# The second half of a gated MLP, and the down projection behind it, one tick later in a hand-ordered selective-scan block

## The chip, the cores and the metric

The kernel runs on one core of a Trainium2 chip. The metric is the device time of one execution in microseconds (us). The core has five engines that matter here: PE (TensorE, matmuls), DVE (VectorE), ACT (ScalarE), POOL (GpSimd) and SP (SyncE, which issues nearly all DMAs). Each engine executes its own instructions strictly in the order in which the program gives them; the engines meet only at semaphores.

## What is computed

The input `x` is 4 sequences of 1024 rows of 256 numbers, all in float32. The block is

```python
x = x + attn(layernorm(x))          # "attn" is a selective-scan (Mamba) layer with its own MLP
x = x + ffn(layernorm(x))

def attn(h0):                       # rmsnorm inside
    h   = h0 + mamba(rmsnorm(h0, n1))
    xn  = rmsnorm(h, n2)
    return h + (silu(xn @ gate.T) * (xn @ up.T)) @ down.T     # gate, up: 704 wide

def mamba(u):                       # z, x, B, C, dt_raw = split(u @ in_proj.T)
    dt = softplus(dt_raw @ dt_proj.T + b)
    state = exp(dt * A) * state + (dt * x) * B                # one step per row, 8 x 32 x 32 states
    y     = sum over states of state * C
    return ((y + x * D) * silu(z)) @ out_proj.T

def ffn(x):                         # 1024 wide; fwht is a Hadamard transform
    return fwht(silu(x @ W1.T) * (x @ W3.T)) @ W2.T
```

The Hadamard transform is folded into `W2` once, at the start of the kernel.

## The kernel before

**Units, steps and ticks.** The work is cut into 8 units of 512 rows (two to a sequence; the second carries the scan's state on). A unit's scan takes 16 steps `q`, each with four scans of 128 partitions by 512 time steps, and each step takes two *ticks*. So a unit is scanned for 32 ticks, and the 8 units are scanned one after the other without a break. What comes before a unit's scan (`pre`: norms, projections, the DMAs that spread dt and dt*x over the partitions) and what follows it (`post`: output projection, the gated MLP, the second norm, the ffn) is laid beside the scans of the units around it.

**What sets the order.** Nothing is scheduled by a planner. `at(tick, lane, fn)` (L264) puts a piece of work in a list, and the loop at L938 to L981 runs through the ticks and empties the lists lane by lane. Within one tick the order of emission is: lane `PE`; lane `ACT`; DVE's product bx = (dt*x)*B (`times_b`, L838); lane `ACTb`; two exponentials `exp` on ACT (L808), for scans two ticks ahead; a scan (L847); lane `DVE`; the second scan; lane `POOL0`; on even ticks POOL's product with C (`times_c`, L860, 4.5 us each); lane `POOL`; on odd ticks the sums over states on PE (`sum_states`, L871: four matmuls that collapse the partitions into the PSUM tile `py`); lane `PEend`; lane `ACTend`; then the DMAs on SP. "Behind the tick's sums" thus means lane `PEend`.

**The sums.** A group of 8 steps accumulates in the one PSUM tile `py`. The group starts with a matmul of x with a diagonal D (L869) and ends when ACT copies `py` out to `yt` (L889); as there is one `py`, the next group's L869 waits for that copy.

**The part that the change touches.** Let F be the tick at which `post` of a unit bases its MLP; the first six units ("many") have F = 33 + 32 times their number. Their MLP runs beside the scan of the next unit:

- F+9, F+10: transposes of the normed rows, `ht` (L239, L246).
- `gated` (L271) computes three 128-wide chunks of silu(gate)*up: gate matmuls for three chunks (`pg`), then one projection `z` of a later unit, then up matmuls (`pu`), two pieces of PE work a tick; `silus` on ACT one tick after the first matmuls (three silus and the one of `z`, with a change of the activation table before and after), copies `up` of the up results one tick later (L296), products on POOL one tick later (L300). A chunk is 128 columns of gate or up; the last is 64 wide and its gate and up come out of one matmul.
- The first three chunks enter at F+10, the second three at F+13 (L718 to L720).
- F+16 to F+22: projections of a later unit that lie in between: C's first half (`pe_c`, emitted at F+16, copied out by ACT as `cc`, L475, at F+17), dt (L447, F+18, lane `PEend`, then softplus on ACT, L456, F+19), C's second half (F+21).
- `down` (L721 to L728, by `add_rows`, L323): four row blocks of 128 rows, each an identity matmul that brings the residual `hr` (L336) and six matmuls over the chunks (L338). They stand at F+18, F+19, F+20 and F+21 in lane `PE`. After the second and after the fourth, ACT copies the sum back to `hr` (`replace`, L352) and takes the norm's statistics (`row_stats`, L193 and L196).
- F+23 to F+26: POOL turns the statistics into a scale (`small3`, L671 and the lines around), ACT norms the rows (`hn`, L226, F+24), PE transposes them (F+25), ACT copies them as `xt`, and the ffn's matmuls begin (F+26).

The six units take different tiles of the same pools: four PSUM banks `dense` for all matmul results but `py`, one SBUF tile each for the MLP's and the ffn's products. A matmul into a `dense` bank waits until the engine that reads the bank's last content is through.

A scan tile `da` is loaded by DMA (dt, spread), overwritten by ACT's exponentials, by DVE's scan and by POOL's product, and read by PE's sums. There are five; the DMA for step q+3 goes to the tile of step q-2, so it waits for that step's sums.

Of the kernel before, what the change touches and what calls it, by code (L numbers as in the profile page):

```python
# [27 lines left out]
def tile_block(ctx: ExitStack, tc: tile.TileContext, a, out):  # L28
# [195 lines left out]
    def scaled_rows(dst, src, scale, bias, ts):  # L224
        for t in ts:
            nc.scalar.activation(  # L226
                dst[:, t, :],
                src[:, t, :],
                AF.Identity,
                bias=bias[:, t : t + 1] if bias is not None else 0.0,  # L230
                scale=scale[:, t : t + 1],
            )
# [15 lines left out]
    def project(w, col, n, src, dst=None):  # L248
        if dst is None:
            dst = dense_psum()  # L250
        for k in range(2):
            nc.tensor.matmul(  # L252
                dst[:n],
                lhsT=w[:, k, col : col + n],
                rhs=src[:, k, :],
                start=(k == 0),
                stop=(k == 1),
            )
        return dst
# [4 lines left out]
    def at(tick, lane, fn, *args):  # L264
        todo[tick][lane].append(partial(fn, *args))
# [5 lines left out]
    def gated(tick, u, dst, wa, wb, chunks, src, z=None):  # L271


        g = [{} for _ in chunks]
        pe_z, act_z = z[0]["z"] if z else (None, None)

        def pe(i, name, w):
            c, n = chunks[i]
            if n < P:

                both = project(W[w], c * P, 2 * n, u[src])
                g[i]["pg"], g[i]["pu"] = both, both[n:]
            else:
                g[i][name] = project(W[w], c * P, n, u[src])

        def silus():
            for i, (_, n) in enumerate(chunks):
                g[i]["si"] = p3.tile([P, T], F32, tag="si", name="si")
                nc.scalar.activation(g[i]["si"][:n], g[i]["pg"][:n], AF.Silu)  # L289
            if z:  # L290
                act_z(z[1])

        def up(i):
            n = chunks[i][1]
            g[i]["up"] = p3.tile([P, T], F32, tag="up", name="up")
            nc.scalar.copy(g[i]["up"][:n], g[i]["pu"][:n])  # L296

        def product(i):
            c, n = chunks[i]
            nc.gpsimd.tensor_tensor(u[dst][c][:n], g[i]["si"][:n], g[i]["up"][:n], ALU.mult)  # L300

        three = len(chunks) == 3
        steps = [(i, *s) for s in (("pg", wa), ("pu", wb)) for i in range(len(chunks))]
        steps = [s for s in steps if chunks[s[0]][1] == P or s[1] == "pg"]
        late = z and len(steps) == 6
        steps = [(pe, *s) for s in steps]
        if z:
            steps.insert(3, (pe_z, z[1]))
        for k, step in enumerate(steps):
            at(tick + k // 2, "PE", *step)  # L310
        at(tick + 1, "ACTend" if three else "ACT", silus)
        at(tick + 2, "ACTend" if z else "ACT", up, 0)
        for i in range(1, len(chunks)):
            if i == 2 and late:
                at(tick + 3, "ACT", up, i)
            else:
                at(tick + 2, "ACTend", up, i)
        at(tick + 3 if z else tick + 2, "POOL", product, 0)
        for i in range(1, len(chunks)):

            at(tick + 3, "POOL" if three or u is not us[-2] else "POOL0", product, i)
# [325 lines left out]
    def post(u, E, other):  # L647


        s = {}  # L650
        last = u is us[-1]

        many = us.index(u) < len(us) - 2

        def hr(ts):
            if 0 in ts:
                u["hr"] = p2.tile([P, TT, DM], F32, tag="hr", name="hr")
            scaled_rows(u["hr"], u["x"], u["r1"], u["nm1"], ts)

        def small2():  # L660
            t = sm.tile([P, 2, TT], F32, tag="s2", name="s2")
            r3 = t[:, 1, :]
            rsqrt_eps(r3, u["mv"][:, 1, :])
            s["r3"] = r3

        def small3():
            t = sm.tile([P, 2, TT], F32, tag="s2", name="s2")
            nm, r4 = t[:, 0, :], t[:, 1, :]
            nm16, var = u["mv"][:, 0, :], u["mv"][:, 1, :]
            rsqrt_eps(r4, var)  # L670
            nc.gpsimd.tensor_tensor(nm, nm16, r4, ALU.mult)  # L671
            nc.gpsimd.tensor_scalar(nm, nm, 16.0, None, ALU.mult)
            s["r4"], s["nm"] = r4, nm

        def hn(scale, bias):
            s["tok"] = p1.tile([P, TT, DM], F32, tag="tok", name="hn")
            scaled_rows(s["tok"], u["hr"], s[scale], s[bias] if bias else None, range(TT))

        def big(name):
            if last:  # L680

                k = NQ + (1 if name == "m" else 3)
                tiles = [das[i % 5] for i in (k, k + 1)]
                u[name] = [tiles[c // 4][:, c % 4, :] for c in range(8)]
            else:
                tile = p1.tile([P, 8, T], F32, tag="big", name=name)
                u[name] = [tile[:, c, :] for c in range(8)]

        def store(lo=0, n=TT):
            b, first = u["b"], u["c"] * T + lo * P  # L690
            nc.sync.dma_start(
                out=out[b, first : first + n * P, :].rearrange("(t p) d -> p t d", p=P),
                in_=u["hr"][:, lo : lo + n, :],
            )

        at(E + 3, "ACT", hr, (0, 1))
        at(E + 4, "ACT", hr, (2, 3))
        add_rows(
            (E + 3,) * TT,
            u,  # L700
            lambda: [u["yt"][:, k, :] for k in range(2)],
            lambda: [W["wo"][:, k, :] for k in range(2)],
            "PEend",
            way="pool" if many else None,
        )
        for i in range(2):
            at(E + (5 + i if many else 4), "ACTend", row_stats, u, "hr", (2 * i, 2 * i + 1), False)

        F = E + 1 if many else E - 2
        at(E + 7 if many else E + 5, "POOL", small2)  # L710
        at(F + 8, "ACT", hn, "r3", None)
        at(F + 9, "PE", lambda: transposes(u, s["tok"]))
        at(F + 9, "ACTend", transposed, u, "ht")
        at(F + 9, "POOL", lambda: nc.gpsimd.tensor_tensor(u["hr"], u["hr"], u["x"], ALU.add))
        at(F + 10, "PE", big, "m")
        sizes = [min(P, DFF - c * P) for c in range(6)]
        chunks = list(enumerate(sizes))
        for i in range(2):  # L718
            gated(F + 10 + 3 * i, u, "m", "wg", "wu", chunks[3 * i : 3 * i + 3], "ht",
                  (other, i) if other else None)  # L720
        down = (18, 19, 20, 21) if many else (17, 17, 18, 18)  # L721
        add_rows(
            [F + t for t in down],
            u,
            lambda: [u["m"][c][:n] for c, n in enumerate(sizes)],
            lambda: [W["wd"][:n, c, :] for c, n in enumerate(sizes)],
            way="pe",
        )  # L728
        at(F + down[1] + 1, "ACTend", row_stats, u, "hr", (0, 1))
        if last:  # L730
            at(F + down[3] + 1, "DVE", row_stats_vector, u, "hr", (2, 3))
        else:
            at(F + down[3] + 1, "ACTend", row_stats, u, "hr", (2, 3))
        at(F + down[3] + 2, "POOL", small3)
        if not many:
            F -= 3
        at(F + 24, "ACTend" if many else "ACT", hn, "r4", "nm")
        at(F + 25, "PE", lambda: transposes(u, s["tok"]))
        at(F + 25, "ACTend", transposed, u, "xt")
        at(F + 26, "PE", big, "g")  # L740
        chunks8 = [(c, P) for c in range(8)]
        for i in range(3):
            gated(F + 26 + 3 * i, u, "g", "w1", "w3", chunks8[3 * i : 3 * i + 3], "xt")

        o2 = (E + 31, E + 36, E + 50, E + 50) if not (many or last) else range(F + 36, F + 40)
        add_rows(
            o2,
            u,
            lambda: u["g"],
            lambda: [w2h[:, c, :] for c in range(8)],  # L750
            way=None if last else "pool",
        )
        if last:
            at(o2[1] + 1, "SPend", store, 0, 2)
            at(o2[3] + 1, "SPend", store, 2, 2)
        else:
            at(o2[3] + 6, "SPend", store)
# [142 lines left out]
    for k, u in enumerate(us):  # L900
        post(u, 32 * k + 32, us[k + 2] if k + 2 < len(us) else None)
# [148 lines left out]
```

## Time and profile before

| | us |
|---|---|
| median of 3 runs | 1126.01 (1125.77 to 1127.81) |
| the profiled execution's own time | 1129.06 |
| its span, from the first to the last instruction | 1127.3 |
| PE busy with matmuls | 980.5 (87%) |
| DVE busy | 943.9 (84%) |
| POOL busy | 882.8 (78%) |
| ACT busy | 805.0 (71%) |
| mean granted clock of PE | 0.925 |
| bx of tick F of units 0 to 6, from the start | 153, 276, 399, 525, 646, 772, 895 |

A fp32 matmul leaves two records, so a group of four matmuls shows as x8. "Busy" says how long an engine had work in it; what matters for the end is which engine makes another one wait, stage by stage. A line of the timeline gives the start and the length of a run of like instructions, and in brackets how long the engine had been idle before it and whose semaphore ended that. Times in it are from the span's start.

### The profile page before, as it was taken

What the parts mean: (1) busy time and instruction counts of PE and PEld (TensorE: products, weight loads), DVE (VectorE), ACT (ScalarE), POOL (GpSimd) and SP (SyncE); (2) the same over time, 40 slices, a digit from 0 to 9 for tenths busy, and PEclk for the clock granted to TensorE, in tenths of its full rate; (3) what the DMA queues carried; (4) which work ended last, traced back from release to release, by engine and by line L of the source; (5) the groups of instructions that cost most, each with busy time, mean ns of one, the idle gap of its engine ahead of it and who ended that gap; (6) DMA issues with size and microseconds to landing.
All of it is one profiled execution on the core that took longest, in us unless ns stands there. A gap on an engine that the chain in (4) does not pass through costs nothing.

```text
span 1127.3 us, 12518 instructions
## 1 busy us (share of the span) xinstructions
PE 980.5 (87%) x3470; PEld 474.4 (42%) x3470; DVE 943.9 (84%) x813; ACT 805.0 (71%) x1443; POOL 882.8 (78%) x512
## 2 busy tenths in 40 slices
PE   7656246979999799989998999979998999898998
PEld 3121012333644345443644354433644363434555
DVE  4899799999989999899999999899989989894000
ACT  3956456887869796888779796979777777584331
POOL 6767668878998899888988899878988788685222
PEclk9777558989999899989999899989999999898999
DMA  7999998998998989998998989899999978760000
GB/s 236 375 363 347 319 377 313 327 317 309 306 342 298 351 302 316 320 333 300 319 347 309 343 284 338 307 337 310 314 321 323 325 255 315 264 223 1 1 19 19
DMA packets 108390, 321.94 MB, mean 286 GB/s; under 512 B 11488, under 2 KB 22176, under 8 KB 108320
## 3 DMA queue, kind: packets, MB, share of 16 engines
q1 hardware_dynamic: 106464, 318.39, 80.8%
q10 hardware_dynamic: 1856, 2.75, 0.7%
q8 instruction: 28, 0.46, 0.2%
q14 instruction: 42, 0.34, 0.1%
HBM read 302.22 MB, written 18.87 MB: 285 GB/s over the span
## 4 chain that ended last, share of the span: by engine, by line
PE 44%; ACT 12%; DMA 7%; DVE 5%; POOL 4%; issue 4%; SPq 0%; DVEq 0%; ACTq 0%; POOLq 0%
PE dense L252 27%; PE dense L338 11%; ACT da L808 5%; DMA da<-dtd 4%; PE py L871 4%; DVE da L847 3%; POOL da L860 3%; DMA ub<-ud 2%; DVE bx L838 2%; ACT up L296 1%; ACT un L226 1%; ACT hr L226 1%; PE dense L336 1%; ACT junk L196 1%; ACT junk L193 1%
## 5 line engine op out<-in xcount | busy, mean ns | idle before, releaser
L860 POOL TENSOR_TENSOR da<-da,cr 128x2048 f32<-128x2048 f32 x128 | 579.2, 4526 | 41.4 <-DVE da L847 19.1
L808 ACT ACTIVATE da<-da,nega 128x512 f32<-128x512 f32 x508 | 335.7, 715 | 72.9 <-DMA da<-dtd 67.3
L838 DVE TENSOR_TENSOR bx<-ub,pb 128x1024 f32<-128x1024 f32 x254 | 312.2, 1229 | 28.5 <-ACT pb L825 11.7
L847 DVE TENSOR_TENSOR_SCAN da<-da,carry,bx 128x512 f32<-128x512 f32 x256 | 313.9, 1267 | 22.0 <-ACT da L808 6.1
L847 DVE TENSOR_TENSOR_SCAN da<-da,bx 128x512 f32<-128x512 f32 x256 | 298.5, 1207 | 17.0 <-DVE bx L838 3.0
L252 PE MATMUL dense<-xt,w 128*128 128x512 f32 x512 | 241.8, 626 | 7.9 <-ACT xt L246 7.9
L871 PE MATMUL py<-da,rsel 128*32 128x512 f32 x1024 | 155.7, 670 | 83.7 <-POOL da L860 83.7
L252 PEld LDWEIGHTS dense<-xt,w 128*128 128x128 f32 x512 | 99.1, 200 | 146.9 <-issue 114.2
L296 ACT COPY up<-dense 128x512 f32<-128x512 f32 x112 | 63.4, 578 | 56.5 <-PE dense L252 56.3
L338 PE MATMUL dense<-w2h,g 128*128 128x256 f32 x448 | 102.1, 383 | 1.2 <-ACT ut L246 1.2
L871 PEld LDWEIGHTS py<-da,rsel 128*32 128x32 f32 x1024 | 23.8, 112 | 179.0 <-POOL da L860 118.4
L338 PEld LDWEIGHTS dense<-w2h,g 128*128 128x128 f32 x448 | 83.5, 190 | 24.2 <-issue 10.4
L300 POOL TENSOR_TENSOR g<-si,up 128x512 f32<-128x512 f32 x56 | 71.0, 1274 | 28.1 <-ACT up L296 28.1
L252 PE MATMUL dense<-ut,win 128*128 128x512 f32 x192 | 92.7, 614 | 0.2 <-ACT ut L246 0.2
L252 PE MATMUL dense<-ht,wg 128*128 128x512 f32 x192 | 87.6, 600 | 3.0 <-ACT ht L246 3.0
L338 PE MATMUL dense<-wd,m 128*128 128x256 f32 x336 | 85.7, 397 | 3.3 <-POOL m L300 3.3
L289 ACT ACTIVATE si<-dense 128x512 f32<-128x512 f32 x112 | 61.9, 595 | 34.9 <-PE dense L252 34.5
L252 PE MATMUL dense<-ht,wu 128*128 128x512 f32 x160 | 73.9, 601 | 1.8 <-ACT si L289 1.8
L300 POOL TENSOR_TENSOR m<-si,up 128x512 f32<-128x512 f32 (+1 forms) x42 | 52.6, 1274 | 26.1 <-ACT up L296 26.1
L338 PEld LDWEIGHTS dense<-wd,m 128*128 128x128 f32 x336 | 63.2, 195 | 21.2 <-issue 9.3
L808 ACT ACT_TABLE_LOAD x46 | 59.0, 1283 | 0.8
L252 PEld LDWEIGHTS dense<-ut,win 128*128 128x128 f32 x192 | 36.8, 197 | 52.5 <-issue 41.0
(110 smaller groups left out, 884.4 us busy)
## 6 DMA issues: line engine op xcount, KB each, us to landing
da<-dtd SPq DMA_DIRECT2D x254, 512.0 KB
ub<-ud SPq DMA_DIRECT2D x254, 512.0 KB
cr<-cd SPq DMA_DIRECT2D x64, 256.0 KB
x<-in_x SPq DMA_DIRECT2D x8, 512.0 KB
dtd<-dt SPq DMA_DIRECT2D x16, 256.0 KB
ud<-du SPq DMA_DIRECT2D x16, 256.0 KB
cd<-cc SPq DMA_DIRECT2D x16, 256.0 KB
xr<-xbd SPq DMA_DIRECT2D x60, 64.0 KB
```

What stands on the lines that cost most here:

```text
L193: nc.scalar.activation(junk, src[:, t, :], AF.Identity, scale=-1.0 / (16 * DM), accum_out=nm)
L226: nc.scalar.activation(dst[:, t, :], src[:, t, :], AF.Identity, bias=bias[:, t : t + 1] if bias is not None else 0.0, scale=scale[:, t : t ...
L252: nc.tensor.matmul(dst[:n], lhsT=w[:, k, col : col + n], rhs=src[:, k, :], start=(k == 0), stop=(k == 1),)
L289: nc.scalar.activation(g[i]["si"][:n], g[i]["pg"][:n], AF.Silu)
L296: nc.scalar.copy(g[i]["up"][:n], g[i]["pu"][:n])
L300: nc.gpsimd.tensor_tensor(u[dst][c][:n], g[i]["si"][:n], g[i]["up"][:n], ALU.mult)
L338: nc.tensor.matmul(dst, lhsT=left[k][:, t * P : (t + 1) * P], rhs=right[k], start=(k == 0 and way != "pe"), stop=(k == n - 1),)
L808: nc.scalar.activation(da, da if q else s["u"]["pdt", b], AF.Exp, scale=an[:, s["h"], s["j"], b, s["g"] : s["g"] + 1],)
L838: nc.vector.tensor_tensor(s["bx"], s["ub", b0 // 2], u["pb"].unsqueeze(1).broadcast_to([P, 2, T]), ALU.mult)
L847: nc.vector.tensor_tensor_scan(da, da, s["bx"][:, b % 2, :], start, ALU.mult, ALU.add)
L860: eng.tensor_tensor(da, da, s["cr"].unsqueeze(1).broadcast_to([P, n, T]), ALU.mult)
L871: nc.tensor.matmul(u["py"][32 * b : 32 * b + 32, :], lhsT=rsel[:, 2 * s["j"] + s["g"], :], rhs=s["da"][:, b, :], start=False, stop=last,)
```

## The change

In the six units with `many`, the second three chunks of the gated MLP enter at F+14 instead of F+13; with them their silus, copies and products and the `z` projection move by one tick. `down`'s row blocks stand at F+19, F+20, F+20 and F+21 instead of F+18, F+19, F+20 and F+21, and in lane `PEend` instead of `PE`. What follows from the ticks in `add_rows` and below moves too: the first `replace` and its statistics go from F+20 to F+21; the second stays at F+22. The last two units are as they were.

```diff
         for i in range(2):
-            gated(F + 10 + 3 * i, u, "m", "wg", "wu", chunks[3 * i : 3 * i + 3], "ht",
+            gated(F + 10 + (4 if many else 3) * i, u, "m", "wg", "wu", chunks[3 * i : 3 * i + 3], "ht",
                   (other, i) if other else None)
-        down = (18, 19, 20, 21) if many else (17, 17, 18, 18)
+        down = (19, 20, 20, 21) if many else (17, 17, 18, 18)
         add_rows(
             [F + t for t in down],
             u,
             lambda: [u["m"][c][:n] for c, n in enumerate(sizes)],
             lambda: [W["wd"][:n, c, :] for c, n in enumerate(sizes)],
+            "PEend" if many else "PE",
             way="pe",
         )
```

The order of the instructions that results, on the four engines' queues and on SP:

- PE, before: pu of chunk 2, pg of chunks 3, 4, 5, z, sums (F+14), pu 3 and 4, C, sums (F+16), row block 0, L869, sums (F+18), dt, row blocks 1 and 2, sums (F+20), C, row block 3, sums (F+22).
- PE, after: pu of chunk 2, pg of chunks 3 and 4, sums (F+14), pg 5, z, C, pu 3 and 4, sums (F+16), L869, sums (F+18), dt, row block 0, sums (F+20), row blocks 1 and 2, C, row block 3, sums (F+22).
- ACT: the silus of chunks 3 to 5 and of z, with their two table changes, stand behind two more exponentials, and the copies `up` of chunks 3 to 5 stand behind two more; the first `replace` with its four statistics instructions stands behind two more.
- POOL: the products of chunks 3 to 5 stand behind the C product of F+17 instead of ahead of it.
- DVE and SP: the same instructions in the same order.

## The prediction

> **What bounds the kernel now.** I read the shares first, then the chain that ended last, then one unit's stage engine by engine, then the clock. No engine is full (PE 87%, DVE 84%), so the chain has to say who makes whom wait.
>
> ```profile
> PE 44%; ACT 12%; DMA 7%; DVE 5%; POOL 4%; issue 4%; SPq 0%; DVEq 0%; ACTq 0%; POOLq 0%
> PE dense L252 27%; PE dense L338 11%; ACT da L808 5%; DMA da<-dtd 4%; PE py L871 4%; DVE da L847 3%; POOL da L860 3%; DMA ub<-ud 2%; DVE bx L838 2%; ACT up L296 1%; ACT un L226 1%; ACT hr L226 1%; PE dense L336 1%; ACT junk L196 1%; ACT junk L193 1%
> ```
>
> PE carries 44% of the chain; from 316 to 909 us it is PE in unit after unit, with pieces of ACT and DMA between. DVE, which the scan keeps nearly full, is the engine that then waits: at tick F+15 of units 1 to 5 its bx stood idle 3.5, 2.2, 1.5, 1.8 and 2.4 us because ACT copied late what PE had made late. So in units 1 to 5 a microsecond of PE delay is a microsecond of time unless a parallel path covers it; unit 0 is not PE's (below). Here is PE's timeline at the changed stage, unit 2 (F+13 to F+26):
>
> ```profile
> 455.23 1.98 PE L252 MATMUL dense<-ht,wu 128*128 128x512 f32 x4
> 457.05 5.31 PE L252 MATMUL dense<-ht,wg 128*128 128x512 f32 x12
> 462.20 1.88 PE L252 MATMUL dense<-ut,win 128*128 128x512 f32 x4
> ...
> 465.01 3.70 PE L252 MATMUL dense<-ht,wu 128*128 128x512 f32 x8
> 468.55 1.88 PE L252 MATMUL dense<-ut,win 128*128 128x512 f32 x4
> 470.36 1.06 PE L871 MATMUL py<-da,rsel 128*32 128x512 f32 x8
> 471.35 0.70 PE L336 MATMUL dense<-hr,ident 128*128 128x256 f32 x2
> 471.89 2.95 PE L338 MATMUL dense<-wd,m 128*128 128x256 f32 x12
> 474.76 1.12 PE L869 MATMUL py<-xr,dd 128*128 128x512 f32 x2
> 476.52 1.16 PE L871 MATMUL py<-da,rsel 128*32 128x512 f32 x8 [0.63 <-POOL da L860]
> ...
> 498.32 2.80 PE L239 MATMUL dense<-ident,hn 128*128 128x128 f32 x8 [2.06 <-ACT hn L226]
> ```
>
> PE is without a gap from 442 to 492 but for the 0.63 us at 476.52. Row block 0 (471.35) lies between the sums that end a `py` group (470.36) and L869, which needs that group copied out. ACT's and POOL's rows of the same stage:
>
> ```profile
> 468.80 1.19 ACT L296 COPY up<-dense 128x512 f32<-128x512 f32 x2 [0.97 <-PE dense L252]
> 471.25 0.59 ACT L475 COPY cc<-dense 128x512 f32<-128x512 f32 x1
> 472.97 0.57 ACT L889 COPY yt<-py 128x512 f32<-128x512 f32 x1
> 497.68 2.06 ACT L226 ACTIVATE hn<-hr,s 128x256 f32<-128x256 f32 x4
> 471.93 4.54 POOL L860 TENSOR_TENSOR da<-da,cr 128x2048 f32<-128x2048 f32 x1
> ```
>
> **The change part by part**, on unit 2.
>
> *PE, up to 471 us.* The same matmuls in another order: two gate chunks from 457.05 (3.54, as the x8 at 465.01), sums (1.0) to 461.6, chunk 5 and z to 465.1, C to 466.9, pu 3 and 4 to 470.4, sums to 471.4. Before they ended at 471.4 too: 0. Do new bank waits open? C's bank comes free with silu 3, which ACT reaches at 460.9 (its exponential of F+14 done) + 1.24 (that of F+15, now ahead) + 1.28 (table) + 0.56 = 464.0, against C at 465.1. The last up matmul needs z's silu, 465.9, against 468.7. 0; if the cover of 1.1 us went, its excess would fall on PE. The exponential of F+15 moves up 5.2 us; its DMA was issued at 447.85, and such loads take some 10 us (issued 496.09, awaited until 506.13), so it has landed.
>
> *POOL.* Products 3 to 5 now stand behind the C product of F+17. That one loses its wait for the copies (POOL idle 4.18 us ahead of 467.91) and starts at about 467.3, when DVE's scan ends, instead of 471.93; the products run 471.9 to 475.6, yt*z to 476.8, the C product of F+19 from 476.8 to 481.4 (before: 482.2). POOL catches up before row block 0 asks: 0 cost. The 0.63 us before the sums of F+18 (0.88, 0.87, 0.62, 0.88 in units 1, 3, 4, 5) goes.
>
> *ACT and L869: the new wait.* The copies for chunks 3 to 5 now come between the last up matmul and yt. ACT: up 4 and 5 from 470.6 (1.1), cc 0.49, two exponentials 1.23, yt 473.4 to 474.0. L869 starts at about 474.1, and PE, with nothing it may run between, is idle 471.4 to 474.1: 2.65 us. Queued behind it on PE are the sums of F+18, dt, all row blocks and the ffn's transposes. Before, row block 0 filled this place; the wait for ACT was there and cost nothing.
>
> *Sum on PE.* L869 474.1 + 1.13, sums 1.10, dt 1.82, row block 0 3.31, sums 1.0, blocks 1 and 2 3.35 + 3.41, C 1.82, block 3 3.31: it ends at 494.35 instead of 492.3: +2.65 - 0.63 = +2.0. From there to the ffn the steps are as before (replace, statistics, `small3`, hn, transposes, 9.2 us), so the first ffn matmul comes 2.0 us late. The first `replace`, moved behind two exponentials, is done by 490, before block 3: 0. The loads of `da` wait for sums: those of F+14 come 3.4 us earlier, F+20 4.7 earlier, F+22 2.0 later, as late as the rest. SP's order is unchanged; its dtd store waits for dt's softplus on ACT, which the longer queue makes 0.4 us later. The exponentials of F+23, behind hn's statistics, come 2.0 us later; DVE's scan used them 3.4 us after they were done here (first one done at 495.9, scan at 499.34), 1.9 in units 1 and 5: 0, just.
>
> *What covers it.* xt also waits, on ACT, behind an exponential that waited for its DMA: 1.24 us in unit 1 (at 377.14), 0.59 in unit 3, 0.94 in unit 4, nothing in 2 and 5. Net per unit: 0.6, 2.0, 1.3, 1.2, 1.8, together 6.9 us. In unit 0 POOL, paced by DVE, released the sums ahead of hn only after a gap of 4.53 us at 246.26, and the statistics were ready 2.7 us before POOL took them up: 0.
>
> *The clock.* Whether the idle 2.65 us also costs clock no row shows at this place. The nearest: stretches with columns span, PE, PEld, DVE, ACT, POOL busy, granted clock.
>
> ```profile
> 494.60:498.10 3.50, 1.16 (x8) 0.26 (x8) 3.37 (x4) 3.47 (x9) 2.72 (x7) 0.99 1.03 371
> 498.10:501.50 3.40, 2.76 (x9) 1.48 (x9) 3.31 (x3) 3.40 (x8) 3.15 (x4) 0.50 1.02 328
> 740.40:743.80 3.40, 1.64 (x16) 0.26 (x8) 3.27 (x4) 3.27 (x11) 2.96 (x3) 1.00 0.91 307
> ```
>
> After a stretch with 2.3 us idle the clock is halved (498.1, for 6.8 us); after one with 1.76 (740.4) it is kept. The clock steps on a grid of 3.4 us, so 2.65 us of idle time halve it when some 2.05 of them fall in one stretch: all but 1.45 of 3.4 us of phases, 0.58 of the units. A halved stretch does 1.7 us less work, sometimes two follow; I take 1.8. Bounds for five units: 0 (never) to 17 (always two stretches); taken 5 x 0.58 x 1.8 = 5.2.
>
> A rule of the Trainium skill speaks against this term: TensorE: Matmul & The Clock Gate, in the section on why this matters for kernels, asks for no PE idle gaps over about 3 us and returns to the half clock after an idle window. By that rule a gap of 2.65 us costs no clock, and the sum would be 6.9 us. The row at 498.1, with 2.3 us idle, differs, and I go by the row.
>
> Total 6.9 + 5.2 = 12.1. On the profiled execution 1129.1 + 12.1 = 1141.2; it stands 3.05 over the median, so 1126.0 + 12.1 = 1138.1.
>
> **The rivals.**
>
> 1. *The gap opens but the clock holds or more of it is covered.* Then 3 to 7 us: 1129 to 1133. For it: 1.76 us of idle time kept the clock; DMA paths run as late as hn in units 1, 3, 4. Against: units 2 and 5 have no cover.
> 2. *Faster: the chain that the change cuts is the one that decides.* The chain of waits runs here from pu 4 over ACT's copies to POOL's product (470.70), its C product (471.97) and PE's sums (476.52). The new order takes products out of it: -0.6 to -0.9 in five units, -3.9 us, 1122. It decides if L869 starts within 0.6 us of the sums' end, so yt would have to be copied by 472.0; ACT's queue after pu 4 adds up to 3.4 us, so I see no way but an ACT much faster than its rows.
> 3. *No change*, the gap in the shadow of a DMA path everywhere: within 2.3 us. Against: DVE's idle time at F+15 of each unit, which PE feeds.
> 4. *Worse*: two halved stretches in each unit and DVE late for F+23's exponentials: 6.9 + 17 = 24 and more, 1150 or above.
>
> **How the numbers follow.** Chances: forecast (1133 to 1147) 0.52, rival 1 0.24, rival 2 0.09, rival 3 0.07, rival 4 0.08. The range 1127 to 1150 leaves out rival 2, part of 3 and rival 4, some 0.2. A measurement here can tell about 0.2% (2.3 us) from no change; so faster 0.09, same 0.07, slower 0.84.
>
> **What would show it.** Right: before L869 in units 1 to 5 an idle PE of about 2.6 us put down to ACT's yt, no wait of the sums behind it; half clock after it in some units; block 3 ending 2 us or more later against the stage's start; more DVE idle time before the next unit's F+15. Wrong: L869 within 0.6 us of the sums; a wait of C for silu 3; hn unmoved because a DMA path decides.

## The result and the profile after

The changed kernel takes 1144.03 us (median of 4 runs, 1141.41 to 1144.37) against 1126.91 us for the kernel before, run beside it. The ratio is 1.0141, with a 95% interval of 1.0112 to 1.0170, so it is 15.9 us slower (12.6 to 19.2; the prediction had 12.1). Its profiled execution took 1141.41 us, the shortest of the four: 12.35 us more than the profiled execution of before. Times in "us against before" below are the ratio less one, times 1128 us.

The chain that ended last, in the profile of the changed kernel; shares of the span by engine, then by line:

```profile
PE 55%; DMA 14%; ACT 13%; POOL 10%; issue 4%; DVE 4%; SPq 0%; ACTq 0%; POOLq 0%; DVEq 0%
PE dense L252 32%; PE dense L338 14%; POOL da L861 7%; PE py L872 6%; DMA da<-dtd 6%; ACT da L809 5%; DMA ub<-ud 3%; DVE da L848 2%; DVE bx L839 1%; ACT hn L226 1%; PE dense L336 1%; DMA cr<-cd 1%; ACT up L296 1%; DMA x<-in_x 1%; ACT un L226 1%
```

PE's share has grown from 44% to 55%, and POOL, ACT and DMA have more of it too. The lines after the changed function are one higher than before: L869 is now L870, L871 is L872, L889 is L890, L860 is L861. PE's timeline in the changed kernel at the stage that the prediction showed, unit 2 (start, length, and in brackets the idle time before and its releaser):

```profile
468.87 3.60 PE L252 MATMUL dense<-ht,wu 128*128 128x512 f32 x8
472.40 1.07 PE L872 MATMUL py<-da,rsel 128*32 128x512 f32 x8
476.12 1.95 PE L870 MATMUL py<-xr,dd 128*128 128x512 f32 x2 [2.66 <-ACT yt L890]
478.00 1.88 PE L872 MATMUL py<-da,rsel 128*32 128x512 f32 x8
...
484.94 1.06 PE L872 MATMUL py<-da,rsel 128*32 128x512 f32 x8
...
495.02 2.95 PE L338 MATMUL dense<-wd,m 128*128 128x256 f32 x12
497.90 1.92 PE L872 MATMUL py<-da,rsel 128*32 128x512 f32 x16
503.93 2.80 PE L239 MATMUL dense<-ident,hn 128*128 128x128 f32 x8 [4.11 <-ACT hn L226]
```

The gap of the prediction is there, 2.66 us ahead of L870. No sums wait behind it. The same gap of 2.65 or 2.66 us stands in all six units, at 222.60, 350.03, 476.12, 602.33, 728.57 and 854.83. ACT's timeline in the same kernel shows why:

```profile
472.56 1.19 ACT L296 COPY up<-dense 128x512 f32<-128x512 f32 x2 [1.13 <-PE dense L252]
473.78 0.58 ACT L475 COPY cc<-dense 128x512 f32<-128x512 f32 x1
474.26 1.33 ACT L809 ACTIVATE da<-da,nega 128x512 f32<-128x512 f32 x2
475.50 0.57 ACT L890 COPY yt<-py 128x512 f32<-128x512 f32 x1
```

`yt` ends at 476.07, behind the copies of the last two ups, C's copy and two exponentials; PE had nothing left at 473.46. The rows of the clock, in the stretches of the changed kernel (columns: span, PE, PEld, DVE, ACT, POOL busy with counts, granted clock, DMA share, GB/s):

```profile
472.90:476.30 3.40, 0.74 (x9) 0.18 (x2) 3.28 (x4) 3.35 (x7) 3.40 (x3) 1.00 0.95 363
476.30:479.70 3.40, 3.40 (x10) 0.40 (x10) 3.16 (x4) 3.30 (x11) 3.40 (x4) 0.50 0.93 262
479.70:483.10 3.40, 3.40 (x15) 2.17 (x12) 3.27 (x4) 3.37 (x5) 3.40 (x1) 1.00 0.93 339
```

The whole gap falls into one stretch of 3.4 us, and the next stretch is granted half clock: L870 and the sums behind it took 1.95 and 1.88 us instead of 1.12 and 1.16. In the trace's record of the clock the half speed of units 1 and 2 begins at 349.99, 377.30, 476.29 and 503.59 us, 8, 29 and 8 times 3.413 us apart. This is the grid on which the clock changes here. The starts at 377.30 and 503.59 lie behind the wait for `hn` and were there before the change too (375.18 and 498.06).

**Where the 12.35 us are.** The first ffn matmul of a unit (L252, from `xt`) comes 1.35 us later than before in unit 0, and 1.96, 5.61, 8.15, 9.34 and 12.41 us later in units 1 to 5. So 11.1 us arise between the ffn of unit 0 and that of unit 5. That stretch in the kernel before, in the columns above, and who made PE wait in it (us in total, times, longest):

```profile
253.70:873.35 619.65, 585.80 (x2140) 286.47 (x2140) 578.40 (x481) 502.82 (x905) 546.79 (x307) 0.97 0.92 319
```

```profile
PE dense L239 <- ACT hn L226: 13.8, 10, 3.1
PE py L871 <- POOL da L860: 10.0, 10, 1.8
PE dense L252 <- ACT xt L246: 6.6, 5, 2.0
...
PE py L869 <- ACT yt L889: 1.6, 4, 0.4
```

The same stretch and the same waits in the changed kernel:

```profile
255.05:885.76 630.71, 589.78 (x2140) 285.81 (x2140) 579.51 (x482) 504.38 (x905) 547.78 (x307) 0.96 0.91 314
```

```profile
PE dense L239 <- ACT hn L226: 20.6, 5, 4.1
PE py L870 <- ACT yt L890: 15.3, 10, 2.7
PE dense L252 <- ACT xt L246: 1.8, 5, 0.4
```

The same 2140 records took 589.78 us instead of 585.80, so 4.0 us are slower matmuls. The rest of the two stretches, 630.71 - 589.78 = 40.9 against 619.65 - 585.80 = 33.9, is idle time: 7.1 us more. By groups, the wait for `yt` is up by 13.7 us and the one for POOL's C product is gone (10.0). Some of the latter has only merged into the wait for `hn` behind it, up by 6.8. The one for `xt` is down by 4.8. These groups name 5.7 of the 7.1.

### The profile page after: what moved, and what is told of

It is laid out like the page before. It is cut to its first block, busy times and chain, and to the rows that moved or that the text cites. A ratio compares the mean times of both kernels' runs of the same rounds, so it can differ in the third digit from the quotient of the medians.

```text
span 1139.6 us, 12517 instructions
## 1 busy us (share of the span) xinstructions
PE 984.1 (86%) x3470; PEld 473.2 (42%) x3470; DVE 944.0 (83%) x813; ACT 806.4 (71%) x1443; POOL 882.3 (77%) x512
## 4 chain that ended last, share of the span: by engine, by line
PE 55%; DMA 14%; ACT 13%; POOL 10%; issue 4%; DVE 4%; SPq 0%; ACTq 0%; POOLq 0%; DVEq 0%
PE dense L252 32%; PE dense L338 14%; POOL da L861 7%; PE py L872 6%; DMA da<-dtd 6%; ACT da L809 5%; DMA ub<-ud 3%; DVE da L848 2%; DVE bx L839 1%; ACT hn L226 1%; PE dense L336 1%; DMA cr<-cd 1%; ACT up L296 1%; DMA x<-in_x 1%; ACT un L226 1%
## 5 line engine op out<-in xcount | busy, mean ns | idle before, releaser
L861 POOL TENSOR_TENSOR da<-da,cr 128x2048 f32<-128x2048 f32 x128 | 579.2, 4525 | 50.4 <-DVE da L848 27.3
L252 PE MATMUL dense<-xt,w 128*128 128x512 f32 x512 | 239.1, 620 | 3.1 <-ACT xt L246 3.1
L872 PE MATMUL py<-da,rsel 128*32 128x512 f32 x1024 | 155.4, 678 | 69.8 <-POOL da L861 69.8
L252 PEld LDWEIGHTS dense<-xt,w 128*128 128x128 f32 x512 | 98.1, 197 | 140.6 <-issue 114.3
L252 PE MATMUL dense<-ut,win 128*128 128x512 f32 x192 | 95.8, 636 | 1.0 <-ACT ut L246 0.9
L872 PEld LDWEIGHTS py<-da,rsel 128*32 128x32 f32 x1024 | 23.6, 113 | 166.6 <-POOL da L861 93.9
L252 PE MATMUL dense<-ht,wg 128*128 128x512 f32 x192 | 89.2, 603 | 3.1 <-ACT ht L246 3.1
L252 PE MATMUL dense<-ht,wu 128*128 128x512 f32 x160 | 73.2, 597 | 1.5 <-ACT si L289 1.5
L252 PEld LDWEIGHTS dense<-ut,win 128*128 128x128 f32 x192 | 37.7, 203 | 52.1 <-issue 41.5
L870 PE MATMUL py<-xr,dd 128*128 128x512 f32 x32 | 25.0, 873 | 36.5 <-ACT yt L890 30.8
```

The lines of the kernel that those rows point to most:

```text
L252: nc.tensor.matmul(dst[:n], lhsT=w[:, k, col : col + n], rhs=src[:, k, :], start=(k == 0), stop=(k == 1),)
L861: eng.tensor_tensor(da, da, s["cr"].unsqueeze(1).broadcast_to([P, n, T]), ALU.mult)
L870: nc.tensor.matmul(u["py"], lhsT=dd[:, s["h"], :], rhs=x, start=True, stop=False)
L872: nc.tensor.matmul(u["py"][32 * b : 32 * b + 32, :], lhsT=rsel[:, 2 * s["j"] + s["g"], :], rhs=s["da"][:, b, :], start=False, stop=last,)
```

## The experiments

**Each part alone.** The first runs undo one of the two edits. In e1 the second three chunks stay at F+14 and `down` is as before.

```diff
-        down = (19, 20, 20, 21) if many else (17, 17, 18, 18)
+        down = (18, 19, 20, 21) if many else (17, 17, 18, 18)
...
-            "PEend" if many else "PE",
```

> Only the second half of the gated MLP is a tick later; the row blocks stand where they did, row block 0 ahead of L869. Theory (PE's new wait for yt ahead of L869, and the clock it costs, are the whole loss): row block 0 fills that place again, but its last three matmuls wait for POOL's products, 1.3 us; L869 finds yt long copied; no halved stretch there. 0 to +4 us against the kernel before. Rival (the later silus, copies and products cost by themselves, by way of ACT and POOL): nearly the whole +12 to +18 us stays.

Measured: 1133.65 us, ratio 1.0054 (1.0035 to 1.0073), +6.1 us against before. PE's timeline of this kernel in unit 2:

```profile
475.69 1.98 PE L338 MATMUL dense<-wd,m 128*128 128x256 f32 x8
478.20 0.70 PE L338 MATMUL dense<-wd,m 128*128 128x256 f32 x2 [0.53 <-POOL m L300]
479.43 0.70 PE L338 MATMUL dense<-wd,m 64*128 64x256 f32 x2 [0.53 <-POOL m L300]
480.06 1.12 PE L869 MATMUL py<-xr,dd 128*128 128x512 f32 x2
```

Row block 0 again fills the place ahead of L869, which waits for nothing. But it stands where POOL has only just made the products: twice 0.53 us, and 2.76 us in unit 0:

```profile
224.90 0.70 PE L338 MATMUL dense<-wd,m 128*128 128x256 f32 x2 [2.76 <-POOL m L300]
```

The loss was larger than expected, and in this profile it lies in unit 0. There the long wait is followed by two halved stretches (226.89 to 233.71), and the first ffn matmul comes 3.8 us later than before, of which the start of the scan accounts for 0.55. From the ffn of unit 0 to that of unit 5 e1 takes 618.87 us, no more than before (619.65). So it is the products behind the C product of F+17 that cost here, but in unit 0; in units 1 to 5 the short waits made the whole no longer. In e2 it is the other way round: `down` as changed, the chunks at F+13.

```diff
-            gated(F + 10 + (4 if many else 3) * i, u, "m", "wg", "wu", chunks[3 * i : 3 * i + 3], "ht",
+            gated(F + 10 + 3 * i, u, "m", "wg", "wu", chunks[3 * i : 3 * i + 3], "ht",
```

> Only the row blocks are later and in lane PEend; the gated MLP is as before. Theory: PE waits for yt ahead of L869 (about 2.2 us, since C's 1.8 us now lie ahead of the sums) and then for POOL's C product of F+17, which stands behind the products again (1.9 us): about 4 us of idle PE in one place, row block 3 some 3.3 us later than before, and the clock halved behind it: worse than both parts together, +18 to +28 us. Rival (the row blocks cost little, the later batch costs): 0 to +5 us.

Measured: 1157.76 us, ratio 1.0263 (1.0242 to 1.0285), +29.7 us, just above what was expected. PE's timeline of this kernel in unit 2:

```profile
482.63 1.12 PE L870 MATMUL py<-xr,dd 128*128 128x512 f32 x2 [2.17 <-ACT yt L890]
485.53 2.03 PE L872 MATMUL py<-da,rsel 128*32 128x512 f32 x8 [1.78 <-POOL da L861]
487.49 3.76 PE L447 MATMUL dense<-raw,dtw 128*128 128x512 f32 x4
```

Two waits in a row, and matmuls at half speed behind them. `down` alone is the costly part. Done together the parts cost 15.9 us, not 6.1 + 29.7. The later second batch puts POOL's C product of F+17 ahead of the products, which takes away the second wait, and the later `down` takes row block 0 away from those products.

**Is it the wait for `yt`?** The next kernel, e3, is the changed one with that copy put ahead of the exponentials of its tick.

```diff
-                at(2 * q + 4, "ACTend", y, u, s["h"])
+                at(2 * q + 4, "ACT" if s["h"] == 0 and 0 < us.index(u) < 7 else "ACTend", y, u, s["h"])
```

> The changed kernel, with the copy of py to yt at F+17 ahead of two exponentials instead of behind them. Theory: L869 starts 1.23 us sooner, PE idles 1.3 to 1.4 us there instead of 2.65, which is under what halves the clock; row block 3 ends 0.7 us later than before: +1 to +4 us against the kernel before, PE's clock at 1.00 behind the gap. Rival (the loss comes from the order elsewhere): +12 us or more stays.

Measured: 1137.15 us, ratio 1.0082 (1.0055 to 1.0108), +9.2 us, more than expected. PE's timeline of this kernel in unit 2:

```profile
477.94 1.12 PE L870 MATMUL py<-xr,dd 128*128 128x512 f32 x2 [1.44 <-ACT yt L890]
...
486.42 1.16 PE L872 MATMUL py<-da,rsel 128*32 128x512 f32 x8 [1.23 <-POOL da L861]
```

The gap is 1.2 us shorter and matmuls behind it run at full clock. But what was won ahead of L870 was handed back at the sums of F+20, which now wait 1.23 us for POOL's C product. The two idle times add up to 2.67 us, as the one did. POOL's path was as late as ACT's: it had been hidden by the gap. So e3 won no idle time; its 6.7 us over the changed kernel (15.9 - 9.2) go with the full clock, which the next run looks at by itself.

**What is the clock worth?** The next kernel, e4, is the changed one with two unread matmuls in the gap.

```diff
+        def filler(n):
+            p = dense_psum()
+            for _ in range(n):
+                nc.tensor.matmul(p, lhsT=ident, rhs=W["wg"][:, 0, 0:T], start=True, stop=True)
+        if many:
+            at(F + 17, "PE", filler, 2)
```

> The changed kernel with two matmuls into a spare bank, whose result nobody reads, between the sums of F+16 and L869. They fill 1.75 of the 2.65 us and change nothing else: L869 still waits for yt, so the order and the lateness stay. Theory with the clock as a cost of its own: the clock stays full, 1.7 us less in each of five units, and +5 to +9 us against the kernel before remain, for the wait alone. Rival (the wait alone is the cost, the clock is beside it): as the changed kernel, +12 to +18 us.

Measured: 1137.29 us, ratio 1.0086 (1.0064 to 1.0107), +9.7 us (7.2 to 12.1), just above what was expected. PE's timeline of this kernel in unit 2 (L733 is the unread pair):

```profile
476.14 1.98 PE L733 MATMUL dense<-wg,ident 128*128 128x512 f32 x4
478.87 1.12 PE L877 MATMUL py<-xr,dd 128*128 128x512 f32 x2 [0.75 <-ACT yt L897]
479.92 1.06 PE L879 MATMUL py<-da,rsel 128*32 128x512 f32 x8
```

L877 and the sums run at full speed behind the pair, and L877 starts 3.73 us after the start of the sums of F+16 (475.14), as in the changed kernel (3.72). So the wait is as long and only the clock differs. Against the changed kernel that is 15.9 - 9.7 = 6.2 us; the ffn of unit 0 to that of unit 5 says the same, 630.71 against 624.55 us. Over that stretch the wait alone then costs 4.9 us (624.55 against 619.65 before). By times alone it is 6 us give or take 4, since each of the two ratios is known to about 2.5 or 3 us.

**Does filling the gap with needed work take the whole loss back?** In e5 C's first half goes behind the sums of F+16, and row block 1 ahead of the sums of F+20, in all six units.

```diff
-        at(H - 15, "PE", pe_c, 0)
+        gap = us.index(u) >= 2
+        at(H - 14 if gap else H - 15, "PE", pe_c, 0)
...
-        at(H - 14, "ACT", act_c, 0)
+        at(H - 13 if gap else H - 14, "ACT", act_c, 0)
...
-        down = (19, 20, 20, 21) if many else (17, 17, 18, 18)
+        down = (19, 19, 20, 21) if many else (17, 17, 18, 18)
```

> The changed kernel with two edits in units 1 to 5's place: C's first half (1.82 us of PE work) moves from ahead of pu 3 and 4 to behind the sums of F+16, and so into the gap ahead of L869, and row block 1 moves ahead of the sums of F+20 (down at F+19, F+19, F+20, F+21), so that these sums are asked for 3.35 us later. Theory (the change costs what ACT's late yt and POOL's late C product leave PE idle, 2.65 us in each unit, and the halved stretch behind it): the gap ahead of L869 shrinks by C's 1.8 us, and a little more or less by the copy of C on ACT, to 0.3 to 1.0 us; the sums of F+20 wait for nothing; no halved stretch there; row block 3 ends within 0.5 us of the kernel before, and the time is within -3 to +3 us of it. Rival (what costs is the later second batch itself: products, loads of da, the first replace): the gap closes and the time stays +8 us or more above before.

Measured: 1125.37 us, ratio 0.9978 (0.9966 to 0.9991), 2.5 us faster than before (1.0 to 3.8). PE's timeline of this kernel in unit 2:

```profile
469.52 1.07 PE L873 MATMUL py<-da,rsel 128*32 128x512 f32 x8
470.52 1.98 PE L252 MATMUL dense<-ut,win 128*128 128x512 f32 x4
472.90 1.12 PE L871 MATMUL py<-xr,dd 128*128 128x512 f32 x2 [0.40 <-ACT yt L891]
...
483.49 1.06 PE L873 MATMUL py<-da,rsel 128*32 128x512 f32 x8
```

The gap is 0.40 us, the sums of F+20 wait for nothing, and the clock holds. All of the loss is gone with the gap and the wait that it hid. The later second batch itself costs nothing once nothing on PE waits for it.

**Is the loss behind hn's gap part of it?** In e7 four unread matmuls go behind the sums of F+24 of the changed kernel.

```diff
+        if many:
+            at(F + 24, "PEend", filler, 4)
```

> The changed kernel with four unread matmuls (3.5 us) behind the sums of F+24, in the place where PE waits 4.11 us for hn. No other instruction moves. Theory (a part of the loss is the clock that this longer wait halves, two stretches in each unit): the idle time there falls to 0.6 us, the clock stays full, hn comes when it came, and PE has up to 3.4 us more work done behind it in each of units 1 to 5: 8 to 15 us less than the changed kernel, so +2 to +9 against the kernel before. Rival (the halved stretches behind hn lie beside other waits and cost nothing): within 2 us of the changed kernel, +15 to +19.

Measured: 1140.98 us, ratio 1.0114 (1.0094 to 1.0133), +12.9 us, 3 us less than the changed kernel, between theory and rival. The intervals of the two ratios overlap, so this is not told from no change; and from the first ffn matmul of unit 1 to that of unit 5 it takes 504.93 us, as long as the changed kernel (504.80). The clock was not kept: behind `hn` one stretch is halved instead of two. Stretches of this kernel in unit 2, in the columns named above:

```profile
502.90:506.30 3.40, 1.98 (x9) 1.17 (x10) 3.27 (x4) 3.40 (x7) 3.15 (x4) 1.00 0.99 387
506.30:509.70 3.40, 3.40 (x5) 1.39 (x5) 3.16 (x4) 3.38 (x6) 3.23 (x3) 0.51 0.90 330
```

The short waits around the transposes (0.48, 0.16 to 0.17, and 0.93 us for `xt`) were enough for one halved stretch.

**One matmul more.** e6 is the changed kernel with one unread matmul at F+20.

```diff
+        if many:
+            at(F + 20, "PE", filler, 1)
```

> The changed kernel with one unread matmul (about 0.88 us of PE work) more in each of the six units, at F+20 ahead of row block 0. Nothing else is moved. Theory (in the changed kernel the distance from one unit's hn gap to the next is a whole number of PE's 3.41 us clock stretches, 37 of them, five times running, because what a unit is late is taken up by a halved stretch that ends on the grid): the distance stays 126.3 us and the time is 0 to +1.5 us against the changed kernel, so +16.5 to +19 against the kernel before. Rival (PE's work simply adds up): +0.88 us in each of five units, so 4.4 us over the changed kernel and +21 to +22.5 against the kernel before, or +17 more where a unit takes 38 stretches.

Measured: 1146.62 us, ratio 1.0164 (1.0140 to 1.0188), +18.5 us, 2.6 us over the changed kernel: between the two. In its trace the first ffn matmuls of units 0 to 5 are 127.49, 126.89, 126.44, 126.33 and 127.96 us apart. Three of them draw near to 126.3 as the theory wants; the last jumps, and the five together are 4.4 us longer than in the changed kernel, as the rival wants. The jump goes with the clock: behind the gap of unit 5 two stretches are halved (857.53 to 864.36), and one in units 1 to 4. By the ratios the 2.6 us are not told from 0 or from 4.4. This settles nothing (see the last section).

**Can the place behind row block 3 be used?** These runs look for a kernel that beats both. First, v1, the kernel before with C's second half behind row block 3.

```diff
-        at(H - 10, "PE", pe_c, 1)
-        at(H - 9, "ACT", act_c, 1)
+        late = 3 if us.index(u) >= 2 else 0
+        at(H - 10 + (2 if late else 0), "PE", pe_c, 1)
+        at(H - 5 if late else H - 9, "ACTend" if late else "ACT", act_c, 1)
```

> The kernel before with C's second half moved from F+21 to F+23, behind row block 3 and into the place where PE waits for hn, and its copy on ACT to F+26. In the kernel before, PE is idle there for 1.75 and 2.06 us in two pieces, so 1.82 us of matmuls fit. Theory (units 1 to 5 are PE-bound from the second batch to the ffn): row block 3, its statistics and hn come 1.8 us earlier in units 1 to 5, less where a DMA of an exponential is the later path (0.6 to 1.2 us in units 1, 3, 4): 0.6 + 1.8 + 1.2 + 0.9 + 1.8 = 6 us at most from this, and fewer halved stretches: -2 to -9 us against before. Rival (hn is set by POOL's small3 or a DMA path, not by row block 3): within 2 us of before, with the idle time ahead of hn's transposes smaller by 1.8 us and their start unmoved.

Measured: 1127.18 us, ratio 0.9989 (0.9976 to 1.0003), -1.2 us, not told from no change. `hn`'s transposes came earlier, but the first ffn matmul then waited for `xt`, 1.02 to 2.29 us in units 1 to 5, and the clock still fell in every unit.

Then v2, which has the edits of e5, v1 and e3 together:

```diff
+        at(H - 14 if gap else H - 15, "PE", pe_c, 0)
...
+        at(H - 10 + (2 if late else 0), "PE", pe_c, 1)
...
+        down = (19, 19, 20, 21) if many else (17, 17, 18, 18)
...
+                at(2 * q + 4, "ACT" if s["h"] == 0 and 0 < us.index(u) < 7 else "ACTend", y, u, s["h"])
```

> e5_gap_filled with C's second half behind row block 3 as in v1_c_behind, and yt copied ahead of the exponentials of its tick. Theory: the gap ahead of L869 is filled by C's first half and by the earlier yt, the one ahead of hn by C's second half, so that both of v1's and e5's gains hold at once: -2 to -11 us against the kernel before, and no more than 1 us slower than v1_c_behind. Rival (the second batch one tick later costs by itself, on POOL and on the loads of da): 4 us or more slower than v1_c_behind.

Measured: 1125.38 us, ratio 0.9974 (0.9958 to 0.9989), -2.9 us. That is close to e5's 2.5 us by itself, and the noise is too large to tell it from the sum of e5's and v1's gains (3.7 us). Then two versions with unread matmuls for the clock's sake. In v4 they go into the kernel before, ahead of `hn`'s transposes; in v3 into v2, ahead of the sums of F+24.

```diff
+            at(F + 24, "PEend", filler, 2)
```

```diff
+            at(F + 24, "PE", filler, 2)
```

> The kernel before with two unread matmuls (1.76 us) behind the sums of F+24, in the place where PE waits 2.04 to 3.08 us for hn and where the clock is halved in each unit. Theory (the halved stretches behind hn make the projection late that DVE waits for at F+15, 1.5 to 3.5 us in units 1 to 5): the clock stays full or falls in fewer units, and the time falls by 3 to 9 us against before; DVE's waits, 11.4 us in all, are the most to be had. Rival (DVE's wait at F+15 comes from elsewhere): within 2 us of before.

> v2_both with two unread matmuls (1.76 us) ahead of the sums of F+24, where PE waits 1.6 to 2.4 us for POOL's C product. Theory: the idle time in any 3.41 us there falls to about 1.5 us, the clock stays full behind it, the waits of DVE at F+15 (1.8, 1.8, 1.6, 1.2, 1.2 us in v2_both) shrink to nothing, and the time falls by 3 to 7 us against v2_both, so -6 to -10 against before. Rival (POOL's path to these sums follows DVE's scan, so that nothing is to be had from PE): within 2 us of v2_both.

Measured: v4 1125.16 us, ratio 0.9972 (0.9959 to 0.9986), -3.2 us; v3 1124.3 us, ratio 0.9974 (0.9961 to 0.9987), -2.9 us, nothing over v2. In v4 the clock was kept in unit 4 alone of units 1 to 5. Stretches of v3 in unit 2:

```profile
495.20:498.60 3.40, 1.70 (x10) 0.41 (x8) 3.27 (x4) 1.60 (x5) 2.91 (x7) 1.00 0.99 389
498.60:502.00 3.40, 2.03 (x7) 1.34 (x8) 3.27 (x4) 2.60 (x6) 3.23 (x3) 0.50 1.02 386
```

The clock fell all the same, in every unit: in the first of these stretches lie a wait of 1.45 us for `hn` and small transposes. The next wait, 1.27 us for `xt`, falls into the halved stretch. The last run, v5, fills both.

```diff
             at(F + 24, "PE", filler, 2)
+            at(F + 24, "PEend", filler, 1)
+            at(F + 25, "PEend", filler, 2)
```

> v3_clock_kept with unread matmuls in the other two waits of that place as well: one (0.88 us) behind the sums of F+24, ahead of hn's transposes (PE waited 1.45 us there in units 1 to 5 of v3_clock_kept), and two (1.76 us) behind the transposes, ahead of the first ffn matmul (1.3 to 2.4 us). Theory (the halved stretches, which v3_clock_kept still had in every unit after 1.7 to 1.9 us of idle time in a stretch, make DVE wait at F+15): the clock stays full in units 1 to 5, DVE's waits there (1.2 to 2.0 us) go, and the time falls by 3 to 8 us against v3_clock_kept, -6 to -11 against before. Rival (the distance of the units is set by POOL and the loads of da, not by PE's clock): within 2 us of v3_clock_kept, though the clock is kept.

Measured: 1117.32 us, ratio 0.9903 (0.9882 to 0.9923), 8.7 to 13.3 us faster than before, and 8 us (by the two ratios) less than v3. PE's timeline of v5 in unit 2 (L736 are the unread matmuls):

```profile
488.93 1.88 PE L736 MATMUL dense<-wg,ident 128*128 128x512 f32 x4
491.46 1.16 PE L884 MATMUL py<-da,rsel 128*32 128x512 f32 x8 [0.65 <-POOL da L873]
492.55 1.12 PE L736 MATMUL dense<-wg,ident 128*128 128x512 f32 x2
494.08 0.33 PE L239 MATMUL dense<-ident,hn 128*128 128x128 f32 x1 [0.40 <-ACT hn L226]
...
496.16 1.88 PE L736 MATMUL dense<-wg,ident 128*128 128x512 f32 x4
498.23 3.70 PE L252 MATMUL dense<-xt,w 128*128 128x512 f32 x8 [0.19 <-ACT xt L246]
```

Its stretch from the ffn of unit 0 to that of unit 5, in the columns above:

```profile
255.00:863.59 608.59, 593.06 (x2191) 287.40 (x2191) 578.47 (x481) 503.09 (x905) 547.87 (x307) 1.00 0.93 325
```

PE is busy for 593.06 us, 7.3 more than before, and yet the stretch is 11.1 us shorter than before: the granted clock is 1.00. The three kinds of wait were not filled one at a time, so which of them is needed stays open. DVE's wait for `pb` at F+15 in units 1 to 5, between 316 and 900 us, fell from 11.7 us before and 8.6 us in v3 to 2.7 us.

## Why the prediction was right, point by point

**The wait, 6.9 us: right in place and path, near in size.** The gap was predicted at 2.65 us and is 2.65 or 2.66 in all units; ACT's order is the predicted one, and `yt` and L870 stand 2.0 us behind the predicted times because unit 1 left the stage 1.96 us late. The wait that was to go, ahead of the sums of F+18, went. The cover was there as well: the DMA wait ahead of `xt` (1.24 us at 377.14 in unit 1) is gone, and with it 4.8 us of PE's waits for `xt`. The idle time of units 1 to 5 rose by 7.1 us. But some of that came with the slow clock: in e4, where the clock is kept at this place, the wait alone costs 4.9 us over the same stretch. Two slips did little harm. Worked unit by unit from its own terms (2.65 us less the wait ahead of the sums and the cover), the prediction's sum is 6.6, not 6.9; and the 0.94 us of unit 4, taken as a DMA's, are put down to DVE's scan in the trace.

**POOL at no cost: right, with no slack at full clock.** The C product of F+19 ends at 483.34 in the changed kernel and the sums of F+20 come at 484.94, so nothing waits; the half clock has made PE the later one there. In e4, at full clock, the two are at 486.09 and 486.15. The prediction's own times, 481.4 against 481.46, said that any gain on ACT would meet POOL next, but the text did not. e3 showed it, and its expectation missed for the same reason.

**Unit 0 at nothing: wrong by 1.1 us.** The gap is there too, and its ffn comes 1.35 us later, of which the start of its scan accounts for 0.3.

**The clock, 5.2 us: near in sum, wrong in both factors.** The prediction took 0.58 of five units at 1.8 us each. The clock fell in six units of six. By e4 the five are worth 6.2 us, so about 1.2 us each. Half speed for 3.4 us holds back 1.7 us of work; that the other 0.5 us would have been lost to later waits in any case is likely, but no run shows it. A share that was too small and a price that was too high nearly cancelled, and that was luck. The share came from the phases of the 3.4 us grid taken as if drawn anew in each unit. They are not: the gap's stretch starts at 346.6, 472.9, 599.2, 725.5 and 851.8, always 126.3 us on, and in each PE is busy for 0.74 to 0.77 us. One unit's phase set all five.

**The rule that spoke against it.** The Trainium skill, TensorE: Matmul & The Clock Gate, in the section on why this matters for kernels, asks for no idle gap above some 3 us. The runs differ: 2.65 us halved the clock six times, and in v3 a gap of 1.45 us, with short ones around the transposes, did so in each of units 1 to 5.

**The sum.** Predicted 12.1; the profiled execution shows 7.1 + 4.0 + 1.3 = 12.4 up to the ffn of unit 5. The median of the four runs lies 6 us above the forecast of 1138.1. The profiles explain the difference only in part. The profiled execution of before was 3.05 us longer than its median, and the forecast took these off; the profiled execution of after was 2.6 us shorter than its own median. What made its other three executions longer, no trace here shows.

**The rivals.** A gap without a loss of clock (rival 1) is what e4 built: 9.7 us, so it would have been above its 3 to 7. The faster case (rival 2) needed `yt` by 472.0; with e3's copy, put ahead of two exponentials, the gap was still 1.44 us. The worse case (rival 4) wanted two halved stretches at this place: there was one in each of units 1 to 5. No change (rival 3) needed the whole gap in the shadow of a DMA path; the waits for `xt` gave back 4.8 of 13.7 us.

## What to carry to other kernels

Price a new wait by its idle time and by the stretches of the clock grid into which it falls, and ask before anything else whether the unit repeats on the grid, since then one phase decides for all units. Before taking a wait away, look for the path that would end next: here ACT's and POOL's were as late as each other, so that shortening one alone (e3) took back no idle time, only the clock, while putting needed work into both places (e5) took back all of the loss. Where PE must wait several times within a few microseconds, unread matmuls in all of the waits kept the clock and were worth some 8 us (v5 against v3). In one of them alone they gave nothing (v3 against v2) to 3 us (v4 against before).

## What the runs showed of the hardware that was not expected

*No single idle time decides the clock.* In the kernel before, a stretch with 1.64 us of PE work kept it (740.4). In v3 one with 1.70 (495.2) and in e7 one with 1.98 (502.9), both with small transposes in it, were followed by half clock. Taken exactly on the grid it is the same: stretches with 1.65 us of PE work (740.41, before) and 1.49 (374.08, e4) kept the clock, and stretches with 1.72 (495.18, v3) and 1.99 (502.94, e7) were followed by half clock. So the prediction's limit, some 2.05 us of idle time in one stretch, is not one: 1.42 us were enough in e7, and 1.92 were not in e4.

*The units' distance sits near whole stretches.* In the changed kernel the first ffn matmuls of units 1 to 5 are 126.14, 126.17, 126.23 and 126.26 us apart, and in e7, where four matmuls a unit were added and PE's idle time was cut, 126.23, 126.23, 126.23 and 126.24: 37 stretches of 3.412 us. With the clock kept, in v5, they are 121.44, 122.60, 121.42 and 121.34, no multiple. A halved stretch ends on the grid, which would pull a PE-bound unit to it. But e6, made to test this, came out between the two answers, so the mechanism stays open.
